# Second layer: the last query projections between sampling tiles, a narrow last tile, and last rows' maxima made inside the third layer's passes

## The chip, the cores and the metric

The kernel runs on one core of one Trainium2 chip. The core has a matmul engine (TensorE, "PE" in the profile, with its weight loads as "PEld"), a vector engine (VectorE, "DVE"), an activation engine (ScalarE, "ACT"), a general engine (GpSimd, "POOL") and a sequencer that issues DMAs (SyncE, "SP"). Each engine works through its own queue in order, and semaphores make one engine wait for another. The metric is the device time of one execution in microseconds.

## What is computed

Two images of 512 channels and 64x64 pixels go through four residual layers, each after a group normalisation `_gn`, all in fp32. The two layers that matter here, cut to their core, are

```python
# layer 1: attention to 256 sampled keys
q   = einsum('oc,bchw->bohw', w_q, x)                # projection, 512 -> 512
off = tanh(w_off2 . gelu(q[::4, ::4] * w_off1 + b_off1)) * 4
kv_feats = grid_sample_bilinear(q, grid + off)       # 16x16 samples for each of 8 heads
k, v = split(w_kv . kv_feats)
x = x + w_out . (softmax(q*scale . k) . v) + b_out
# layer 2: mixture of max pools
x = _gn(x)
s = relu(w2 . relu(w1 . mean(x) + b1) + b2)          # one number per channel
x = x_in + frac_b * maxpool(x, k_b) + frac_s * maxpool(x, k_s) + x    # k in 1,3,...,13
```

"The second layer" of the title is layer 1, "the third" is layer 2.

## The kernel before

The image is held in SBUF as X, 128 channels by 4 chunks (`KC`) by 4096 pixels; a second buffer of the same size, Y, holds what a layer makes on the way. Pixels are handled in 8 blocks (`NB`) of 512 (`TB`), that is, 8 rows of 64. [...]The two images run one after the other through all four layers, in one program. The order of the instructions on each engine is set by a scheduler that follows the order in which the Python code emits them, with priorities of its own; in places the code fixes it.

**Sampling** (`query_and_sample`, L1249). The bilinear sampling is a matmul. `query(blk)` (L1259) projects one block: for each of the 4 output chunks, 4 matmuls (`project`, the matmul is L134), then ACT evacuates the bank into Y (L1264); at the end DVE takes the absolute maximum of the block, `top` (L1267). A tile `t` is 128 pixels, two rows of the image; there are 32. For each tile:

- ACT makes |y - t| for all heads and keys (L1297), DVE turns it into the tent (L1298) and multiplies it by the tent in x, `hatx` (L1299). The result `wt` has two buffers.
- PE transposes the 4 chunks of the tile's queries (L1302) into one of four PSUM banks, ACT copies them to `q_tok` (L1305), which has two buffers as well.
- PE adds the tile to the samples in `acc`, 8 matmuls (L1308), one for each head.

An offset is at most 4 grid steps, so a tile can only touch some of the 16 rows of keys; `keys_near(t)` gives them, and L1297 to L1308 work on that slice of the keys. The first and the last tile take all 16 rows. The loop (L1287) emits the projections of block `blk + 1` ahead of the four tiles of block `blk`. After the last tile one copy takes all samples from PSUM to `feats` (L1310), from which keys and values are made (L1064, L1070).

**End of layer 1** (L1090 to L1122). The attended values of a block stand in Y. `add_output` (L1190) multiplies them by `w_out`, 4 matmuls for each output chunk (L1195), adds the result into X (L1198) and takes the statistics (L1200); L1114 aggregates a chunk's. Meanwhile the 3x3 maxima of X, the first pool of layer 2, are made into Y: `maxima_across` (L1124) makes the horizontal maxima of a block's 8 rows into `rows3` on DVE (L1132, L1134) and copies edges and the two last rows of the block before on ACT (L1131, L1133), `maxima_down` (L1138) the vertical ones on DVE (L1145, L1146, at the very end L1148). Then `pool_mixture` (L1150) turns the statistics of all channels into 7 weights per channel, a chain of small steps on PE, DVE, POOL and ACT (L1157 to L1188). The last `maxima_down`, of three chunks, is issued behind it with `issue_after`.

**Layer 2** (`pool_chunk`, L1337), once for each of the 4 chunks. 8 PSUM banks hold the chunk's image. Seven terms are added into them: term 0 is X itself, term 1 the 3x3 maxima in Y, and terms 2 to 6 are wider maxima. A term is added with 8 matmuls (L1356) by a diagonal of weights that ACT makes (L1361). A wider maximum is made from the last one by two passes of `spread_max` (L689): each is one DVE operation over the whole image (L698) and an ACT copy of its two edges (L699). The passes write in turn to the scratch image `pool_h` and to a buffer of `self.pools`, two of its own and the Y chunks that are free. Behind the last term ACT evacuates the 8 banks into X (L1398), sums squares (L1402) for the next normalisation. In the last chunk these are L1390 and L1391; there the last bank's products of terms 0 to 4 are kept back and issued during term 5, and six weight blocks of layer 3 are scaled on DVE (L978).

Of the kernel before, what the change touches and what calls it, by code (L numbers as in the profile page):

```python
# [933 lines left out]
class Net(General):  # L934
# [102 lines left out]
    def layer1(self, X, Y, d):  # L1037

        tc, nc, vec = self.tc, self.nc, self.vec
        with tc.tile_pool(name="l1", bufs=1) as sp:  # L1040
            wkv = sp.tile([P, KC, 2 * C], F32, name="wkv1")
            nc.sync.dma_start(wkv, d["w_kv1"].rearrange("(kc p) o -> p kc o", p=P))
            wq = sp.tile([P, KC, C], F32, name="wq1")
            feats = sp.tile([P, KC, NK], F32, name="feats")
            bq = sp.tile([P, KC], F32, name="bq1")
            with tc.tile_pool(name="l1a", bufs=1) as wp, \
                    tc.tile_pool(name="l1p", bufs=4, space=PSUM) as pp, \
                    tc.tile_pool(name="l1k", bufs=1, space=PSUM) as ppk:
                grid = wp.tile([P, 2, NK], F32, name="grid")
                nc.sync.dma_start(grid, d["grid"])  # L1050
                top = sp.tile([P, KC, NB], F32, name="top_q")
                self.query_and_sample(X, Y, wq, bq, grid, feats, top, wp, pp, ppk)
            self.ahead = ExitStack()
            dp = self.ahead.enter_context(tc.tile_pool(name="diags", bufs=1, side="right"))
            self.diags = cycle([dp.tile([P, P], F32, name=f"diag{i}") for i in range(2)])
            with tc.tile_pool(name="l1c", bufs=1) as late:

                keys = late.tile([P, KC, NK], F32, name="keys")
                vals = late.tile([P, 2, C], F32, name="vals")
                with tc.tile_pool(name="l1q", bufs=4, space=PSUM) as pp:  # L1060
                    for oc in range(KC):
                        ps = pp.tile([P, TB], F32, name="mm")
                        for kc in range(KC):
                            nc.tensor.matmul(ps[:, :NK], wkv[:, kc, oc * P:(oc + 1) * P],  # L1064
                                             feats[:, kc, :], start=(kc == 0), stop=(kc == KC - 1))
                        nc.scalar.mul(keys[:, oc, :], ps[:, :NK], HD ** -0.5)
                    for t in range(2):
                        ps = pp.tile([P, TB], F32, name="mm")
                        for kc in range(KC):
                            nc.tensor.matmul(ps, feats[:, kc, t * P:(t + 1) * P], wkv[:, kc, C:],  # L1070
                                             start=(kc == 0), stop=(kc == KC - 1))
                        nc.vector.tensor_copy(vals[:, t, :], ps)
                    self.product_bound(top, keys, sp, pp)
                with tc.tile_pool(name="l1b", bufs=2) as wp, \
                        tc.tile_pool(name="l1s", bufs=6, space=PSUM) as pp, \
                        tc.tile_pool(name="l1o", bufs=2, space=PSUM) as ppo:
                    st = wp.tile([P, KC, NB, 6], F32, name="gn_st1", bufs=1)
                    w1 = wp.tile([P, KC, 32], F32, name="w1", bufs=1)
                    nc.sync.dma_start(w1, d["w1"].rearrange("(kc p) e -> p kc e", p=P))
                    w2 = wp.tile([32, C], F32, name="w2", bufs=1)  # L1080
                    nc.sync.dma_start(w2, d["w2"])
                    wo = wp.tile([P, KC, C], F32, name="wo1", bufs=1)
                    nc.sync.dma_start(wo, d["w_out1"].rearrange("(kc p) o -> p kc o", p=P))
                    steps = [(blk, cc) for blk in range(NB) for cc in range(KC)]
                    part = lambda blk, cc=slice(0, KC): Y[:, cc, blk * TB:(blk + 1) * TB]
                    flat = lambda a: a.rearrange("p k o -> p (k o)")
                    probs, totals, later = {}, {}, []
                    rows3 = flat(wkv)[:, :KC * 10 * W].rearrange("p (k y x) -> p k y x", k=KC, x=W)
                    ring = cycle([a[:, n:n + TB] for a, lo, hi in (
                        (flat(wq), 0, KC), (flat(wkv), 5, 8), (flat(feats), 0, 2),  # L1090
                        (wp.tile([P, 3 * TB], F32, name="totals", bufs=1), 0, 3))
                        for n in range(lo * TB, hi * TB, TB)]).__next__
                    for i in range(len(steps) + 4 + KC):
                        if i < len(steps):
                            blk, cc = steps[i]
                            probs[i], totals[i] = self.exponentials(part(blk, cc), keys[:, cc, :],
                                                                    ring, wp, pp)
                        if 1 <= i <= len(steps):
                            blk, cc = steps[i - 1]
                            self.attended(part(blk, cc), probs.pop(i - 1),  # L1100
                                          vals[:, :, cc * P:(cc + 1) * P], ppo)
                        at = lambda n: i >= n and (i - n) % KC == KC - 1 and (i - n) // KC
                        if (blk := at(1)) is not False and blk < NB:
                            r = self.inverse_sums([totals.pop(KC * blk + n) for n in range(KC)], wp,
                                                  pp)
                        if (blk := at(2)) is not False and blk < NB:
                            self.divided(part(blk), r, pp)
                        if (blk := at(3)) is not False and blk < NB:
                            later += [(blk, oc) for oc in range(KC)]
                        if later:  # L1110
                            blk, oc = later.pop(0)
                            self.add_output(X, wo, part(blk), blk, oc, st, pp)
                            if blk == NB - 1:
                                nc.vector.bn_aggr(self.mv[:, oc, :],  # L1114
                                                  st[:, oc].rearrange("p b s -> p (b s)"))
                                self.maxima_across(X, blk, rows3, slice(oc, oc + 1))
                            elif oc == KC - 1:
                                self.maxima_across(X, blk, rows3, slice(0, KC))
                                self.maxima_down(Y, blk, rows3, slice(0, KC))
                    self.maxima_down(Y, NB - 1, rows3, slice(0, 1))  # L1120
                    with tc.issue_after(self.pool_mixture(w1, w2, wp, pp)):
                        self.maxima_down(Y, NB - 1, rows3, slice(1, KC))  # L1122

    def maxima_across(self, X, blk, h, ks):  # L1124

# [12 lines left out]
    def maxima_down(self, Y, blk, h, ks):  # L1138
# [8 lines left out]
        if blk == NB - 1:  # L1147
            nc.vector.tensor_tensor(out[:, :, W - 1], h[:, :, rows], h[:, :, rows + 1], ALU.max)  # L1148

    def pool_mixture(self, w1, w2, sp, pp):  # L1150

        nc, vec, mv = self.nc, self.vec, self.mv
# [6 lines left out]
        nc.vector.tensor_tensor(cent, mv[:, :, 0], ps[:, :KC], ALU.subtract)  # L1159
        nc.vector.tensor_tensor(var, cent, cent, ALU.mult)  # L1160
        nc.vector.tensor_tensor(var, var, mv[:, :, 1], ALU.add)
        ps = pp.tile([P, TB], F32, name="mm")
        nc.tensor.matmul(ps[:, :KC], self.grp, var, start=True, stop=True)
        nc.vector.tensor_scalar(var, ps[:, :KC], 1e-5, None, ALU.add)
# [20 lines left out]
        nc.vector.tensor_tensor(up, up, down, ALU.min)  # L1185
        nc.vector.tensor_scalar(up[:, :5], up[:, :5], 0.0, None, ALU.max)
        nc.vector.tensor_tensor(wts, up, bcast(rstd, 1, 7), ALU.mult)
        return nc.vector.scalar_tensor_tensor(c0, wts[:, 0], 1.0, rstd, ALU.add, ALU.add).ins  # L1188

    def add_output(self, X, w, att, blk, oc, st, pp):  # L1190

# [57 lines left out]
    def query_and_sample(self, X, Y, wq, bq, grid, feats, top, wp, pp, ppk):  # L1249
# [35 lines left out]
            nc.gpsimd.tensor_copy(wq[:, kc], w[:, kc])  # L1285
        in_turn(self.grid_steps(banks, bq, grid, ycoord, hatx, wp, pp), query(0))
        for blk in range(NB):  # L1287
            if blk + 1 < NB:
                in_turn(query(blk + 1))
            for t in range(blk * NT, (blk + 1) * NT):  # L1290

                near = self.keys_near(t) if 0 < t < n_t - 1 else slice(0, 16)
                some = lambda a: a.rearrange("p g (i j) -> p g i j", j=16)[:, :, :, near]
                wt = wp.tile([P, NH, NK], F32, name="wt", bufs=2)
                nw = NK // 16 * (near.stop - near.start)
# [10 lines left out]
                for g in range(NH):  # L1306
                    cc, lo = g // 2, (g % 2) * HD
                    nc.tensor.matmul(some(acc[:, :, :NK])[lo:lo + HD, cc], q[:, g * HD:(g + 1) * HD],  # L1308
                                     wt[:, g], start=(t == 0), stop=(t == n_t - 1))
        nc.vector.tensor_copy(feats, acc[:, :, :NK])  # L1310

    def keys_near(self, t):

# [23 lines left out]
    def pool_chunk(self, X, Y, cc, c0, d0, wts, sp):  # L1337
# [5 lines left out]
        if cc == 0:  # L1343
            self.scratch = sp.tile([P, N], F32, name="pool_h")
            self.pools = [sp.tile([P, N], F32, name=f"pool{i}") for i in range(2)]
        else:
            self.pools.insert(0, Y[:, cc - 1, :])
        h = image(self.scratch)
        accs, kept = self.accs, []
# [1460 lines left out]
```

## Time and profile before

| | us |
|---|---|
| median of 3 runs | 5054.05 (5054.01 to 5058.16) |
| the profiled execution's own time | 5046.35 |
| span of its trace | 5044.5 |
| PE busy | 4804.4 (95%) |
| DVE busy | 3073.6 (61%) |
| ACT busy | 1817.5 (36%) |
| POOL busy | 1848.7 (37%) |
| sampling, last block of projections begins to first key matmul, image 0 | 1183.28 to 1217.57 |
| last `w_out` matmuls begin to first pool matmul, image 0 | 1475.49 to 1509.15 |
| layer 2's matmuls L1356, image 0 | 1509.15 to 1709.4 |

The three lower rows are times from the start of the span; image 1 repeats them about 2506 us later. In a timeline a row is: start, duration, engine, line, operation, out<-in, shapes, count, and in brackets how long the engine sat idle before it and whom it waited for. An fp32 matmul of this kernel is recorded as two instructions; a transpose as one. Matmuls are pipelined, so the durations of neighbours overlap: what counts is the distance of their starts, 0.43 us for one record of 512 columns.

### The profile page before, as it was taken

How to read it: one execution, taken by the hardware profiler on the slowest of the kernel's cores; microseconds unless marked ns; L12 is line 12 of the kernel's file. 1: busy time of each engine (PE TensorE's matmuls, PEld its weight loads, DVE VectorE, ACT ScalarE, POOL GpSimd, SP SyncE). 2: the span in 40 equal slices, each digit the busy share in tenths (PEclk: the TensorE clock that was granted, in tenths of full speed). 3: DMA queues.
4: the chain of work that ended last, by engine and by line, in shares of the span. 5: the costliest groups of instructions: out<-in, count | busy, mean ns of one | idle time of the engine just before them, and what ended most of it. 6: DMA issues, size and time to landing. Idle time of an engine off the chain costs nothing. (4 is left out here: it accounts for less than half of the span.)

```text
span 5044.5 us, 48001 instructions
## 1 busy us (share of the span) xinstructions
PE 4804.4 (95%) x17027; PEld 1980.2 (39%) x17027; DVE 3073.6 (61%) x3994; ACT 1817.5 (36%) x3479; POOL 1848.7 (37%) x1218
## 2 busy tenths in 40 slices
PE   7999999999999999999999999999999999999998
PEld 3433332554334444433343333335543344444333
DVE  4267777754679533478733677777436794335776
ACT  1245655334323233322112555552443232333221
POOL 0036666501320045454500466664013201554554
PEclk9999999999999999999999999999999999999999
DMA  3035556600000000211120355565000000000111
GB/s 153 0 85 145 150 148 173 163 19 10 1 1 17 2 1 1 68 58 44 58 74 0 101 148 150 146 178 142 19 10 1 17 1 1 1 1 24 40 46 44
DMA packets 124172, 307.72 MB, mean 61 GB/s; under 512 B 20818, under 2 KB 33618, under 8 KB 122388
## 3 DMA queue, kind: packets, MB, share of 16 engines
q1 hardware_dynamic: 123924, 304.58, 20.9%
q8 instruction: 136, 2.23, 0.2%
q14 instruction: 112, 0.92, 0.1%
HBM read 256.01 MB, written 48.50 MB: 60 GB/s over the span
## 5 line engine op out<-in xcount | busy, mean ns | idle before, releaser
L134 PE MATMUL mm<-big,w 128*128 128x512 f32 x2496 | 1169.7, 611 | 30.3 <-DVE big L2404 11.8
L134 PEld LDWEIGHTS mm<-big,w 128*128 128x128 f32 x2496 | 453.3, 192 | 712.7 <-issue 550.6
L2613 POOL TENSOR_TENSOR late<-late,big 128x1024 f32<-128x1024 f32 x194 | 460.1, 2371 | 233.4 <-DVE big L2608 202.0
L2447 DVE TENSOR_TENSOR prods<-qs,big 128x1024 f32<-128x1024 f32 (+1 forms) x200 | 334.2, 1686 | 76.5 <-PE tap L2474 66.3
L1643 POOL TENSOR_TENSOR big<-big 128x512 f32<-128x512 f32 x224 | 277.7, 1272 | 219.1 <-ACT big L1634 219.1
L2608 DVE TENSOR_TENSOR big<-big,mm 128x512 f32<-128x512 f32 x388 | 254.8, 682 | 120.0 <-ACT mm L2600 117.0
L2600 ACT COPY mm<-big 128x512 f32<-128x512 f32 x432 | 248.0, 597 | 109.9 <-DMA big<-rows 62.7
L1634 ACT ACTIVATE big<-mm,ed 128x256 f32<-128x256 f32 x512 | 194.1, 490 | 233.0 <-DVE top L1630 200.3
L2518 POOL TENSOR_TENSOR late<-late 128x512 f32<-128x512 f32 x84 | 105.4, 1275 | 429.8 <-ACT late L2503 408.0
L2613 POOL TENSOR_TENSOR late<-late,tap 128x1024 f32<-128x1024 f32 x94 | 222.1, 2363 | 99.6 <-DVE tap L2608 80.6
L1446 POOL TENSOR_TENSOR wq<-prob 128x512 f32<-128x512 f32 x48 | 70.8, 1497 | 502.6 <-ACT prob L1443 502.6
L1898 PE MATMUL mm<-k,w 128*128 128x512 f32 x512 | 238.5, 610 | 12.4 <-DVE k L1891 7.4
L1630 DVE TENSOR_REDUCE top<-mm 128x1 f32<-128x512 f32 x256 | 159.0, 684 | 148.1 <-PE mm L1561 148.1
L134 PE MATMUL mm<-big,wq 128*128 128x512 f32 x512 | 232.4, 603 | 2.7 <-ACT off_t L1223 2.7
L1195 PE MATMUL mm<-big,wo 128*128 128x512 f32 x512 | 234.7, 604 | 0.0
L1608 PE MATMUL mm<-w,big 128*128 128x512 f32 x512 | 234.5, 601 | 0.0
L1356 PE MATMUL acc<-big,diag 128*128 128x512 f32 x512 | 226.8, 600 | 4.6 <-ACT diag L1361 4.6
L973 POOL TENSOR_TENSOR group_stats<-group_stats,cst 128x1 f32<-128x1 f32 (+1 forms) x20 | 12.1, 621 | 560.1 <-DVE group_stats L972 499.9
L1888 DVE RECIPROCAL psD<-psD 128x512 f32<-128x512 f32 x64 | 215.1, 3362 | 1.9
L134 PE MATMUL mm<-big,big 128*128 128x512 f32 x464 | 201.7, 594 | 0.5 <-DVE b_sr L1011 0.5
L1443 ACT ACTIVATE prob<-mm 128x512 f32<-128x512 f32 x256 | 133.0, 602 | 171.3 <-PE mm L1440 171.1
L1530 POOL TENSOR_TENSOR sq<-k 128x512 f32<-128x512 f32 x128 | 132.9, 1040 | 155.4 <-ACT k L1528 139.4
(419 smaller groups left out, 8219.4 us busy)
## 6 DMA issues: line engine op xcount, KB each, us to landing
big<-rows SPq DMA_DIRECT2D x432, 256.0 KB, 4.1
tap<-rows SPq DMA_DIRECT2D x208, 256.0 KB, 4.1
yd<-late SPq DMA_DIRECT2D x32, 512.0 KB, 3.1
lost_all<-lost SPq DMA_DIRECT2D x128, 128.0 KB, 3.1
out<-big SPq DMA_DIRECT2D x64, 256.0 KB, 2.0
big<-in_W_kv SPq DMA_DIRECT2D x8, 1024.0 KB, 10.7
rows<-late SPq DMA_DIRECT2D x64, 128.0 KB, 3.5
big<-in_x SPq DMA_DIRECT2D x32, 256.0 KB, 3.7
```

Source lines behind the costliest of these rows:

```text
L134: self.nc.tensor.matmul(ps, w[:, kc, :], X[:, kc, blk * TB:(blk + 1) * TB], start=(kc == 0), stop=(kc == KC - 1))
L1195: nc.tensor.matmul(ps, w[:, kc, oc * P:(oc + 1) * P], att[:, kc, :], start=(kc == 0), stop=(kc == KC - 1))
L1356: nc.tensor.matmul(accs[b], dg, src[:, b * TB:(b + 1) * TB], start=(j == 0), stop=(j == 6))
L1608: nc.tensor.matmul(ps, X[:, kc, lo:lo + P], wv[:, kc, :], start=(kc == 0), stop=(kc == KC - 1))
L1634: nc.scalar.activation(f[:, t, :], pS[h][i][:, t % 2, :], AF.Exp, bias=ed[:, t, 2 * cc + h:2 * cc + h + 1])
L1643: nc.gpsimd.tensor_tensor(a, a, part, ALU.add)
L1888: nc.vector.reciprocal(psD, psD)
L1898: nc.tensor.matmul(ps, self.wo[:, kc, oc * P:(oc + 1) * P], qs[:, kc, :], start=(kc == 0), stop=(kc == KC - 1))
L2447: self.nc.vector.tensor_tensor(self.pair(u, k)[:, :n].rearrange("p k (y x) -> p k y x", x=W), bcast(qs.rearrange("p (y x) -> p y x", x=W), ...
L2600: nc.scalar.copy(ps, part)
L2608: nc.vector.tensor_tensor(part.rearrange("p (y x) -> p y x", x=W), self.vx[:, y:y + self.UY // 2, dx:dx + W], ps.rearrange("p (y x) -> p y ...
L2613: nc.gpsimd.tensor_tensor(out, out, t, ALU.add)
```

## The change

In the sampling loop the projections of the last block (block 7) are no longer emitted ahead of the tiles of block 6, but one output chunk ahead of each of these four tiles. The last tile takes only its near keys, as the middle ones do. The copy from PSUM to `feats` is made in four pieces, one per chunk.

At the end of layer 1 the maxima of the last block are made for chunk 0 only, between the two parts into which `pool_mixture` is now divided; of block 6 they are made for chunks 0 and 1 only. What is missing (the last 9 rows of chunk 1, the last 17 of chunks 2 and 3) is made in layer 2 by a new function, `maxima_below`, at the start of the chunk that needs it. `issue_after` goes.

```diff
                             if blk == NB - 1:
                                 nc.vector.bn_aggr(self.mv[:, oc, :],
                                                   st[:, oc].rearrange("p b s -> p (b s)"))
-                                self.maxima_across(X, blk, rows3, slice(oc, oc + 1))
-                            elif oc == KC - 1:
+                                if oc < 2:
+                                    self.maxima_across(X, NB - 2, rows3, slice(oc, oc + 1))
+                                    self.maxima_down(Y, NB - 2, rows3, slice(oc, oc + 1))
+                            elif oc == KC - 1 and blk < NB - 2:
                                 self.maxima_across(X, blk, rows3, slice(0, KC))
                                 self.maxima_down(Y, blk, rows3, slice(0, KC))
+                    mixture = self.pool_mixture(w1, w2, wp, pp)
+                    next(mixture)
+                    self.maxima_across(X, NB - 1, rows3, slice(0, 1))
                     self.maxima_down(Y, NB - 1, rows3, slice(0, 1))
-                    with tc.issue_after(self.pool_mixture(w1, w2, wp, pp)):
-                        self.maxima_down(Y, NB - 1, rows3, slice(1, KC))
+                    next(mixture)
...
+    def maxima_below(self, x, to, h, blk):
+        nc = self.nc
+        x, to, h = (a.rearrange("p (y x) -> p y x", x=W) for a in (x, to, h))
+        y = blk * TB // W - 1
+        n = W - y
+        x, h, to = x[:, y - 1:], h[:, y - 1:], to[:, y:]
+        nc.vector.tensor_tensor(h[:, :, 1:W - 1], x[:, :, :W - 2], x[:, :, 2:], ALU.max)
+        nc.scalar.copy(h[:, :, 0:W:W - 1], x[:, :, 1:W - 1:W - 3])
+        nc.vector.tensor_tensor(h, h, x, ALU.max)
+        nc.vector.tensor_tensor(to[:, :n - 1], h[:, :n - 1], h[:, 2:], ALU.max)
+        nc.vector.tensor_tensor(to[:, :n - 1], to[:, :n - 1], h[:, 1:n], ALU.max)
+        nc.vector.tensor_tensor(to[:, n - 1], h[:, n - 1], h[:, n], ALU.max)
...
         nc.vector.tensor_tensor(var, var, mv[:, :, 1], ALU.add)
+        yield
         ps = pp.tile([P, TB], F32, name="mm")
         nc.tensor.matmul(ps[:, :KC], self.grp, var, start=True, stop=True)
...
-        return nc.vector.scalar_tensor_tensor(c0, wts[:, 0], 1.0, rstd, ALU.add, ALU.add).ins
+        nc.vector.scalar_tensor_tensor(c0, wts[:, 0], 1.0, rstd, ALU.add, ALU.add)
+        yield
...
         for blk in range(NB):
-            if blk + 1 < NB:
-                in_turn(query(blk + 1))
+            ahead = query(blk + 1) if blk + 1 < NB else iter(())
+            if blk < NB - 2:
+                in_turn(ahead)
             for t in range(blk * NT, (blk + 1) * NT):
-
-                near = self.keys_near(t) if 0 < t < n_t - 1 else slice(0, 16)
+                next(ahead, None)
+
+                near = self.keys_near(t) if t else slice(0, 16)
...
-        nc.vector.tensor_copy(feats, acc[:, :, :NK])
+            for _ in ahead:
+                pass
+        for cc in range(KC):
+            nc.vector.tensor_copy(feats[:, cc], acc[:, cc, :NK])
...
             self.pools = [sp.tile([P, N], F32, name=f"pool{i}") for i in range(2)]
         else:
+            self.maxima_below(x2, Y[:, cc, :], self.scratch, NB - 1 if cc == 1 else NB - 2)
             self.pools.insert(0, Y[:, cc - 1, :])
```

## The prediction

> **What bounds the kernel now.** First the busy shares: PE is busy 95% of the span, so time is won only where PE stands still, or where its work shrinks. Then the timeline around the two places of the change, image 0. The end of sampling, in the timeline of all engines (start, duration, engine, line, [idle before, releaser]):
>
> ```profile
> 1183.28 11.43 PE L134 MATMUL mm<-big,wq 128*128 128x512 f32 x26
> ...
> 1204.09 0.99 PE L1308 MATMUL acc<-wt,q_tok 128*64 128x112 f32 x16 [1.41 <-DVE wt L1299]
> ...
> 1207.01 2.00 ACT L1297 ACTIVATE wt<-ycoord,yneg 128x2048 f32<-128x2048 f32 x1 [0.48 <-PE acc L1308]
> ...
> 1209.04 1.23 DVE L1298 TENSOR_SCALAR wt<-wt 128x2048 f32<-128x2048 f32 x1 [1.41 <-ACT wt L1297]
> 1210.30 2.29 DVE L1299 TENSOR_TENSOR wt<-wt,hatx 128x2048 f32<-128x2048 f32 x1
> ...
> 1212.74 3.52 PE L1308 MATMUL acc<-wt,q_tok 128*64 128x256 f32 x16 [3.41 <-DVE wt L1299]
> ...
> 1216.30 1.22 DVE L1310 COPY feats<-acc 128x1024 f32<-128x1024 f32 x1 [3.70 <-PE acc L1308]
> ...
> 1217.57 7.17 PE L1064 MATMUL mm<-feats,wkv 128*128 128x256 f32 x32 [1.32 <-DVE feats L1310]
> ```
>
> PE spends its last projections in one dense block; then tiles 26 to 31 come bare, each a chain ACT tent, two DVE steps, PE. From 1197.85 to 1217.57 the windows give PE 12.19 of 19.72 us, at a granted clock of 0.74. The end of layer 1, PE alone:
>
> ```profile
> 1500.18 0.59 PE L1157 MATMUL mm<-channels_mv,cst 128*128 128x4 f32 x2 [7.26 <-DVE channels_mv L1114]
> ...
> 1509.15 15.86 PE L1356 MATMUL acc<-big,diag 128*128 128x512 f32 x32 [2.30 <-ACT diag L1361]
> 1524.84 20.97 PE L1356 MATMUL acc<-pool,diag 128*128 128x512 f32 x48
> 1547.53 7.11 PE L1356 MATMUL acc<-pool,diag 128*128 128x512 f32 x16 [1.72 <-DVE pool L698]
> 1556.35 7.11 PE L1356 MATMUL acc<-pool,diag 128*128 128x512 f32 x16 [1.72 <-DVE pool L698]
> ```
>
> PE stands 7.26 us because DVE is late with statistics: it has maxima in between (DVE timeline: L1132 2.21, L1134 2.28, L1145 2.28, L1146 2.23 us, so the second of the last block's sums, ready at 1485.8, is added at 1490.83). In layer 2 PE waits twice for a pool pass, later never. But DVE is busy 182.95 of layer 2's 200.20 us, and in chunk 1 it already waits for an edge copy that stands in ACT's queue behind the evacuations of chunk 0:
>
> ```profile
> 1566.49 4.29 DVE L698 TENSOR_TENSOR pool_h<-big 128x3968 f32<-128x3968 f32 x1 [1.49 <-ACT big L699]
> ```
>
> [...]at 1509.15 the first five weight loads are 0.86 us apart, then 0.43, which cost 2.1 us.[...]
>
> **The change, part by part**, for one image. The order of each queue is read from the built program: PE's order changes only in the sampling tail, POOL's and SP's not at all, no DMA moves; DVE and ACT change there, at the end of layer 1 and in layer 2.
>
> (a) *Sampling tail.* From 1183.28 PE has 13 projection matmuls left (0.86 each, 11.2), now with tiles 24, 25, 26 among them (4 transposes 0.45 plus 16 records 0.95 each, 4.2) and some 0.25 of waits for q_tok, which stands behind the evacuation (0.69) on ACT: the block ends at 1198.9 instead of 1194.5, three tiles further. Transposes 1.4; tile 27, whose tent is ready, runs 1200.45 to 1201.35, tile 28 to 1202.2. Then bare: tents 29 and 30 on ACT (0.94 each, two buffers, so each behind a PE tile) end 1202.35 and 1203.25; DVE, free at 1202.4 after `top`'s 2.29, makes 0.56+0.96 twice, to 1203.95 and 1205.45; PE 1204.05 and 1205.55. Tile 31 with 80 instead of 256 columns a head: tent 0.84 (from 0.94 and 1.04 at 96 and 112), starting 1205.0; DVE 0.49+0.82; PE 1207.4 to 1208.3. It had cost 2.00+1.23+2.29+3.52. A quarter of the feats copy is 0.42 (L1654, 256 columns, 421 ns), so the key matmuls start at 1208.95: 8.6 earlier. [...]0 or the 2.1 above; I take 2.1. Gain 6.5.
>
> (b) *End of layer 1.* Block 6's maxima come down from four chunks to two, block 7's to one, and stand where DVE waited. After its L1482 (1478.4) DVE has 2.6 us of maxima, then two sums and statistics (1.4 each) to 1483.9, 1.6 of maxima and a statistic, and meets the sum ready at 1485.8 in time, likewise 1489.2. The last, 1492.65, finds DVE free; 0.75+0.69+0.37 less overlap give 1494.5, and L1157 starts at 1494.6: 5.6 earlier. 0.25 more goes because L1146 and L1148 no longer stand ahead of L1159. First pool matmul: 1503.3, 5.85 earlier. The added ACT copies there are 0.25 to 0.30, next to 4 us pauses: nothing.
>
> (c) *Layer 2.* Count from its first matmul, T=0. Removed ahead of the passes: L1145, L1148, L1146 of three chunks, 3.66 us, so the first pass starts at -0.55 instead of +3.11. Added: `maxima_below`, [...]0.80+0.82+0.69+0.22+0.69=3.2 us for chunk 1 (10 rows) and 1.32+1.36+1.22+0.22+1.22=5.3 for chunks 2 and 3 (18 rows), 13.9 in all. A pass is 4.40 start to start, a term's matmuls 6.87. Chunk 0: pass 6 must wait until PE has read term 2 (22.6), +1.2; pass 10 ends 44.6, so term 6 runs 44.65 to 51.5 (before 54.1; the two stalls of 1.72 shrink to about 1.5). Chunk 1 on: queued on ACT behind eight evacuations and four squares (as the copy shown above is) there is now the edge copy of the chunk's *first* pass, and DVE's second pass waits for it: it starts 3.35 after PE has ended the chunk before (1566.49 against 1563.29, and 0.15 for the longer copy). From there to the end of pass 10 are 39.5 (chunk 2 before, less its wait), then term 6 on PE. So each chunk goes round a loop of 3.35+39.5+0.05+6.87=49.8 us, where PE alone needs 48.05: chunk 1 ends at 101.3 (before 102.2), chunk 2 at 151.1 (150.3). Chunk 3: pass 6 ends 176.35, PE waits 1.1; pass 8 ends 185.2, PE waits 2.5; term 5 and the products kept back are 26 records, 11.2, to 196.4; the six scalings L978 (2.5) now stand ahead of pass 10, which ends 196.45. The last term starts at 196.5, before at 193.2 (1702.38): 3.3 lost. The cover that would make (c) free is PE's work, and it is 1.75 too short per chunk.
>
> *Sum:* 6.5+5.85-3.3=9.05 an image, 18.1 for two. The profiled execution, 5046.35 with a span of 5044.5, would become 5028.3; the median stood 7.7 above it and is taken to move alike: 5054.05-18.1=**5036.0**.
>
> **Rivals.**
> *DVE keeps ahead in layer 2*, if edge copies get out sooner: then chunk 0 gives 2.6 more and nothing is lost, 6.5+5.85+2.6=15, twice 30: 5024. For it: DVE's 17 us of slack; against it: ACT's order.
> *The tail stays bare.* If the tiles among projections stall PE on q_tok[...], (a) gives half, 3.3: 5042. For it: 0.81 to 1.59 us pauses at tiles 26 to 30; against it: all operands of 24 to 28 are timely by (a).
> *Layer 2 eats (b) and more.* If below-steps and squares cost 3 us more by chunk 3: 2x(6.5+5.85-8.5)=7.7: 5046.
> *Slower.* The loop of (c) again, as the one bound: if the first edge copy waits for all eight squares, four more at 0.9 put 3.6 on each of three loops, and the six weight scalings of 2.5 then fall whole on the path: 3.3+10.8+2.5=16.6 against 12.35 gained, twice 4.3 lost[...]: 5063 to 5075, say 5065. It decides from 9.05 us an image, 3 us a chunk, beyond my loop. Against it: four squares stood ahead before, and stand ahead now.
> *The change doing nothing* is out: the built program has the narrow tile and the new order.
>
> **How the numbers follow.** Forecast 0.50 (own range 5030 to 5041[...]), DVE ahead 0.17, bare tail 0.14, eaten 0.13, slower 0.06. A range of 5024 to 5046 leaves about 2 in 10 outside. 0.2% is 10 us, about what a measurement of this kernel can tell from no change: faster, 5044 and less, is the first three, 0.81; same is "eaten" and a little of "slower", 0.14; slower 0.05.
>
> **What would show it.** Right: L1064 some 8 us earlier against the last projection block; L1157's wait from 7.26 to under 2; L698's second pass of chunks 1 to 3 released by ACT L699; PE waiting on L698 about 2 us at each chunk's last term, last term near 196.5 after the first matmul. Wrong: no PE wait on L698 in chunks 1 to 3 (then faster), or waits of 5 us there (then slower).

## The result and the profile after

| | before | after |
|---|---|---|
| median of 7 runs, us | 5054.05 (5050.58 to 5058.16) | 5038.71 (5037.15 to 5044.18) |
| ratio after/before, 95% interval | | 0.9969 [0.9959, 0.9978] |
| the profiled execution's own time, us | 5046.35 | 5044.18 |
| span of its trace, us | 5044.5 | 5042.3 |

The kernel became 15.3 us faster; the interval reaches from 11.1 to 20.7. The forecast was 5036.0 with 18.1 to win. But the two profiled executions differ by 2.2 us only: that of before was shorter than each of the seven runs behind its median, that of after the longest of its seven. So these two spans can't be compared; stages can. All kernels of this study have the same number of matmul records (17027), so a stage can be measured between the same records in each trace:

- A: from the record that stands 208 records ahead of the first key matmul (it belongs to a sampling tile, and starts 2.5 us before the row of 26 projections with which the prediction begins) to the first key matmul (L1064);
- B: from there, so with the key matmuls, to the first pool matmul of layer 2;
- C: from there to the first matmul of layer 2's last term;
- rest: everything else in the run but for some 50 us behind C in each image.

| us, image 0 / image 1 | A | B | C | rest |
|---|---|---|---|---|
| before | 36.83 / 36.16 | 291.57 / 291.57 | 193.24 / 193.24 | 3901.3 |
| after | 28.56 / 28.56 | 288.33 / 288.69 | 199.57 / 199.54 | 3908.4 |
| after less before | -8.27 / -7.60 | -3.24 / -2.88 | +6.33 / +6.30 | +7.1 |
| as predicted | -8.6 | -5.85 + 2.1 = -3.75 | +3.3 | 0 |

The 2.1 us that the prediction took off its gain from sampling would be paid in the key matmuls, so in B. The stages give 5.2 and 4.2 us, 9.4 in all, where the forecast said 9.05 for each image. The total came out near the forecast; the sum of its stages is half of it.

**The sampling tail.** The timeline of all engines, kernel after, image 0:

```profile
1208.42 0.88 PE L1330 MATMUL acc<-wt,q_tok 128*64 128x96 f32 x16 [0.82 <-DVE wt L1321]
...
1209.89 0.88 PE L1330 MATMUL acc<-wt,q_tok 128*64 128x96 f32 x16 [0.58 <-DVE wt L1321]
...
1211.73 0.78 PE L1330 MATMUL acc<-wt,q_tok 128*64 128x80 f32 x16 [0.97 <-DVE wt L1321]
1212.54 1.42 DVE L1335 COPY feats<-acc 128x256 f32<-128x256 f32 x4 [0.96 <-PE acc L1330]
...
1213.02 7.17 PE L1064 MATMUL mm<-feats,wkv 128*128 128x256 f32 x32 [0.52 <-DVE feats L1335]
```

The bare tiles are down to three with pauses below 1 us, the wide one (2.00 + 1.23 + 2.29 + 3.52) is gone, and the key matmuls wait 0.52 for a quarter of `feats` instead of 1.32 for all of it. They take 7.17 us, as before, 0.22 us from start to start behind the first (0.32).

**The end of layer 1.** The same view some 250 us later:

```profile
1461.50 2.94 POOL L1472 TENSOR_TENSOR wq<-prob 128x512 f32<-128x512 f32 x2 [5.70 <-ACT wkv L1137]
1461.59 1.73 DVE L1136 TENSOR_TENSOR wkv<-big 128x496 f32<-128x496 f32 x1
...
1463.41 1.57 DVE L1138 TENSOR_TENSOR wkv<-wkv,big 128x512 f32<-128x512 f32 x1
...
1466.29 0.66 DVE L1136 TENSOR_TENSOR wkv<-big 128x496 f32<-128x496 f32 x1
...
1467.66 3.36 DVE L1497 RECIPROCAL recip<-mm 128x256 f32<-128x256 f32 x2
...
1471.08 1.14 PE L1505 MATMUL mm<-recip,cst 2*128 2x512 f32 x8 [1.14 <-DVE recip L1497]
```

Block 6's horizontal maxima (L1136, L1138) stand ahead of the last reciprocals on DVE. The first pair takes 1.73 and 1.57 us, while POOL works on two inputs of its own; the second, with POOL at rest, 0.66 and 0.69. The reciprocals come late and PE stands for 1.14 us. Before, it didn't wait there, and what followed ran at full rate:

```profile
1474.42 1.14 PE L1479 MATMUL mm<-recip,cst 2*128 2x512 f32 x8
...
1475.49 17.43 PE L1195 MATMUL mm<-big,wo 128*128 128x512 f32 x40
```

What follows on PE in the kernel after, to the end of layer 2:

```profile
1472.15 19.13 PE L1215 MATMUL mm<-big,wo 128*128 128x512 f32 x40
1493.26 0.39 PE L1175 MATMUL mm<-channels_mv,cst 128*128 128x4 f32 x2 [1.98 <-DVE channels_mv L1114]
...
1501.35 16.77 PE L1382 MATMUL acc<-big,diag 128*128 128x512 f32 x32 [2.29 <-ACT diag L1387]
...
1547.16 7.10 PE L1382 MATMUL acc<-pool,diag 128*128 128x512 f32 x16 [1.58 <-DVE pool L698]
...
1597.08 7.11 PE L1382 MATMUL acc<-pool,diag 128*128 128x512 f32 x16 [1.62 <-DVE pool L698]
...
1647.02 25.13 PE L1382 MATMUL acc<-big,diag 128*128 128x512 f32 x58 [1.63 <-DVE big L698]
...
1688.14 5.22 PE L1382 MATMUL acc<-pool,diag 128*128 128x512 f32 x8 [2.43 <-DVE group_stats L972]
...
1700.92 7.03 PE L1382 MATMUL acc<-big,diag 128*128 128x512 f32 x16
```

The 7.26 us wait is down to 1.98. The last 40 `w_out` records take 19.13 us instead of 17.43: four of them run at half rate, 0.85 us from start to start instead of 0.43, behind the 1.14 us stall. Such half-rate records behind a stall are called a restart below. In layer 2 PE now waits for DVE at the last term of chunks 0, 1 and 2 (1.58, 1.62, 1.63 us), before only in chunk 0, and twice in chunk 3 (0.97 and 2.43; before once, 0.79). After the 2.43 us eight records take 5.22 us; in before, unstalled, they take 3.68. The ten passes of a chunk (L698, two for each wider maximum) are counted as pass 1 to pass 10. On DVE, in chunk 1 and at the end of chunk 3:

```profile
1557.43 4.29 DVE L698 TENSOR_TENSOR big<-pool_h 128x3968 f32<-128x3968 f32 x1 [2.79 <-ACT pool_h L699]
```

```profile
1693.06 2.46 DVE L978 TENSOR_SCALAR w<-w,group_stats 128x512 f32<-128x512 f32 x6 [0.75 <-POOL group_stats L973]
1695.45 4.28 DVE L698 TENSOR_TENSOR big<-pool_h 128x3968 f32<-128x3968 f32 x1
```

The second pass waits for ACT's edge copy, queued behind evacuations and squares (2.79 here, 0.68 in chunks 2 and 3), and the six weight scalings stand ahead of the last pass. Still, that pass ends at 1699.7 and the last term starts at 1700.92: in this profile the scalings cost nothing, since PE itself was later.

### The profile page after: what moved, and what is told of

It is laid out like the page before. It is cut to its first block, busy times and chain, and to the rows that moved or that the text cites. A ratio compares the mean times of both kernels' runs of the same rounds, so it can differ in the third digit from the quotient of the medians.

```text
span 5042.3 us, 48033 instructions
## 1 busy us (share of the span) xinstructions
PE 4811.1 (95%) x17027; PEld 1980.8 (39%) x17027; DVE 3078.9 (61%) x4020; ACT 1814.7 (36%) x3477; POOL 1858.9 (37%) x1218
## 5 line engine op out<-in xcount | busy, mean ns | idle before, releaser
L973 POOL TENSOR_TENSOR group_stats<-group_stats,cst 128x1 f32<-128x1 f32 (+1 forms) x20 | 20.2, 1027 | 564.6 <-DVE group_stats L972 508.2
```

## The experiments

| run | median, us | ratio to before [95%] | A | B | C |
|---|---|---|---|---|---|
| s_only: sampling part alone | 5035.47 | 0.9966 [0.9954, 0.9978] | 28.56 / 28.55 | 291.56 / 291.57 | 193.56 / 193.46 |
| m_only: maxima part alone | 5053.66 | 0.9995 [0.9986, 1.0003] | 36.74 / 36.46 | 287.10 / 288.22 | 199.27 / 198.17 |
| b0: after, no `maxima_below` | 5024.27 | 0.9942 [0.9929, 0.9956] | 28.55 / 28.55 | 287.00 / 288.86 | 191.87 / 191.57 |
| ds: after, squares later | 5036.63 | 0.9965 [0.9953, 0.9977] | 28.55 / 28.56 | 288.37 / 288.68 | 194.49 / 194.52 |
| w: after, maxima behind the reciprocals | 5035.39 | 0.9964 [0.9950, 0.9978] | 28.55 / 28.57 | 285.59 / 285.59 | 198.18 / 199.23 |
| dsaw: ds and w, statistics on ACT | 5027.56 | 0.9944 [0.9930, 0.9957] | 28.57 / 28.55 | 287.43 / 287.45 | 196.21 / 196.54 |
| dsawk: dsaw, kept products earlier | 5022.59 | 0.9936 [0.9922, 0.9949] | 28.55 / 28.56 | 287.42 / 285.59 | 191.96 / 191.78 |
| n_only: narrow tile alone | 5049.85 (one) | | 31.44 / 30.40 | 293.34 / 291.56 | 193.20 / 193.23 |
| i_only: projections between tiles alone | 5053.77 (one) | | 35.61 / 35.61 | 291.55 / 293.43 | 193.19 / 193.21 |
| before2: before once more | 5052.37 (one) | | 36.67 / 36.83 | 291.56 / 291.56 | 193.21 / 193.23 |

A ratio is to runs of before made along with the run, with medians from 5053.14 to 5055.69. "(one)" is a single execution, of which only the stages are used.

**The two halves.** `s_only` is before with the sampling hunks of the diff, `m_only` before with the others.

> The kernel before with the sampling part alone (last projections between the tiles, narrow last tile, feats in four pieces). Prediction on record: 6.5 us an image, 13.0 in all, 5041. Theory from the trace after: [...]8.3 and 7.6 us in the two images, 15.9 in all, 5038; block of projections to first key matmul 26.0 us in both images. Rival: the gain read from the sampling stage is partly given back behind it (the tiles moved early only shift work): under 10, over 5044.

> The kernel before with the maxima part alone (block 6 and 7 maxima of the chunks split, the rest made in layer 2). Prediction on record: (b) 5.85 less (c) 3.3, that is 2.55 us an image faster, 5049. Theory from the trace after: 3.25 won before the first pool matmul and 6.3 lost behind it, 3.1 us an image slower, 5060. Rival: the two parts help each other and the maxima part alone is neutral, 5054.

The sampling part alone gives all of A and leaves B and C as they were: 15.9 us by A over the two images (8.27 and 7.61). The maxima part alone can't be told from no change by its median; by stages it wins 4.5 and 3.4 in B and loses 6.0 and 4.9 in C, 1.6 us lost an image, half of what the theory from the trace after expected. In image 0 that is because the restart described next did not come. In image 1 the key matmuls took 8.62 us instead of 7.17, which lies in B, and C was 1.1 us shorter. C of after, m_only and w, whose layer 2 is the same code, shows why: it is 199.2 to 199.6 in the four images where half-rate records followed the 2.43 us stall, and 198.2 in the two where they didn't; there the last term waited 0.34 us for pass 10. The neutral rival was nearest, and (c) is larger than (b), which the forecast had the other way round. By medians `s_only` and the whole change can't be told apart; nothing shows that the second half helped.

`m_only` has the same 1.1 us wait at the reciprocals as the kernel after. Its PE timeline:

```profile
1475.47 1.14 PE L1500 MATMUL mm<-recip,cst 2*128 2x512 f32 x8 [1.13 <-DVE recip L1492]
1476.54 17.43 PE L1215 MATMUL mm<-big,wo 128*128 128x512 f32 x40
```

Here the 40 records run at full rate. Over after, b0, ds and m_only, two images each, the wait was followed by half-rate records in five cases and not in three, with the same code. What decides between the two was not shown. The wait was 1.12 to 1.14 us in all eight; where there was no wait (before, before2, s_only, n_only, i_only, w, dsaw and dsawk, 16 cases) all 40 records ran at full rate.

**What of the sampling part does what.** Two more runs: `near = self.keys_near(t) if t else slice(0, 16)` alone (n_only), and the generator `ahead` alone (i_only).

> The kernel before with the narrow last tile alone. By the rows of the bare last tile (2.00 + 1.23 + 2.29 + 3.52 us wide against 0.84 + 0.49 + 0.82 + 0.9 narrow) block of projections to first key matmul 28.3 instead of 34.3 us: 6.0 us an image, 5042. Rival, [...]2 us of it come back, and L1064's 32 records last 9 instead of 7.2 us.

> The kernel before with the last projections between tiles alone, last tile wide and feats in one copy. What the rows of the narrow tile (6.0) and the four pieces of feats (0.8) leave of the 8.27 us of the sampling part: 1.5 us an image, 32.8 us from block to key matmuls. Rival, on record as 'the tail stays bare': nothing, 34.3 us, since tiles 29 to 31 hang on ACT and DVE all the same.

Against A's mean of 36.6 in the four images of before, the narrow tile gives 5.2 and 6.2, the order alone 1.0. The wait ahead of the key matmuls is 0.8 shorter with the four copies, which were not run alone. With 6.2 that makes 8.0 of the 8.1 of the whole part; with 5.2 it falls short. PE's timeline of `n_only`, image 0, shows where it lost 1 us before the key matmuls and more in them:

```profile
1206.19 1.55 PE L1308 MATMUL acc<-wt,q_tok 128*64 128x96 f32 x16 [0.48 <-DVE wt L1299]
1208.42 1.55 PE L1308 MATMUL acc<-wt,q_tok 128*64 128x96 f32 x16 [0.68 <-DVE wt L1299]
1210.17 1.34 PE L1308 MATMUL acc<-wt,q_tok 128*64 128x80 f32 x16 [0.20 <-DVE wt L1299]
1212.83 8.95 PE L1064 MATMUL mm<-feats,wkv 128*128 128x256 f32 x32 [1.32 <-DVE feats L1310]
```

The tiles take 1.55 and 1.34 us instead of 0.88 and 0.78, and the key matmuls 8.95 instead of 7.17: 1.8 us more, where the prediction had charged 2.1. In image 1 of the same run the key matmuls took 7.17. In `i_only` it was image 1 that took longer (9.04). With both parts together, over the seven profiles that have them (s_only, after, b0, ds, w, dsaw, dsawk), the key matmuls took 7.17 in 11 of 14 images and 8.80 to 8.84 in the other 3.

**What layer 2 pays.** `b0` takes out the line that calls `maxima_below` for chunks 1 to 3:

```
-            self.maxima_below(x2, Y[:, cc, :], self.scratch, NB - 1 if cc == 1 else NB - 2)
```

> The kernel after without the three calls of maxima_below (it leaves out the last rows' 3x3 maxima of chunks 1 to 3). Theory that DVE's added 13.9 us are what layer 2 pays: passes keep ahead of PE, last term about 190.5 us after the first pool matmul instead of 199.6, 9 us an image, 5020.5. Rival, that the place of the edge copy in ACT's queue is what costs, not the work: only the waits change hands, last term at 196 to 197, 5032.

C falls by 7.7 and 8.0 us to 191.9 and 191.6, near the 190.5 of the first theory: the work of `maxima_below`, its DVE steps with their edge copy, is what C pays. The rival that only the copies' place matters (196 to 197) falls in this form. But how much of the 13.9 us of work shows depends on the queues, and `ds` moves nothing but those: `finish` makes the squares and statistics of a chunk within the next one.

```
+        def finish():
+            nc.scalar.mul(shift, sums[:, 0, 0:1], -1.0 / TB)
+            for b, xx in enumerate(blocks):
+                nc.scalar.activation(self.junk, xx, AF.Square, bias=shift, accum_out=sums[:, 1, b:b + 1])
...
+            if j == 2 and cc:
+                self.finish()
```

> The kernel after, with the squares of chunks 0 to 2 emitted after the next chunk's first wide maximum, so that on ACT the edge copy of the first pass stands ahead of nearly all squares, and on DVE the six scalings stand behind the last pass. Theory that ACT's order costs DVE 2.8 + 0.7 + 0.7 us an image and the scalings 2.5 more: last term at about 192 instead of 199.6 after the first pool matmul, 7 us an image, 5024.5. Rival, that DVE's work alone (49.3 us a chunk in chunks 2 and 3 against PE's 48.05) is the bound: under 2 us an image, 5035 to 5038. Third: the statistics of chunk 2 come late and stall chunk 3: slower than the kernel after.

C falls by 5.1 and 5.0 us with all of `maxima_below` in place; the waits for edge copies are gone, the scalings stand behind the last pass. It is less than the 7 of the theory. By its median, 5036.63 where 5024.5 was expected, `ds` can't be told from the kernel after. The third rival, late statistics, shows in the trace, though C did not become longer than in after. PE in chunk 3:

```profile
1672.85 0.39 PE L965 MATMUL acc<-channels_mv,cst 128*128 128x3 f32 x2 [2.17 <-DVE channels_mv L1437]
...
1686.15 0.39 PE L970 MATMUL acc<-group_stats,cst 128*128 128x3 f32 x2 [0.79 <-DVE group_stats L968]
...
1697.63 7.03 PE L1382 MATMUL acc<-big,diag 128*128 128x512 f32 x16
```

The statistics of chunk 2 are a chain of six tiny steps, spread among 4.3 us passes on DVE: it begins at 1663.86 and ends at 1681.69. Started later, its third step holds up PE by 2.17 us. The 0.79 us was there in before too.

**The reciprocals.** `w` holds the early maxima back on DVE:

```
                                 if oc < 2:
-                                    self.maxima_across(X, NB - 2, rows3, slice(oc, oc + 1))
-                                    self.maxima_down(Y, NB - 2, rows3, slice(oc, oc + 1))
+                                    with tc.issue_after(self.scaled.ins):
+                                        self.maxima_across(X, NB - 2, rows3, slice(oc, oc + 1))
+                                        self.maxima_down(Y, NB - 2, rows3, slice(oc, oc + 1))
...
-            nc.vector.tensor_tensor(att[:, cc, :], att[:, cc, :], ps, ALU.mult)
+            self.scaled = nc.vector.tensor_tensor(att[:, cc, :], att[:, cc, :], ps, ALU.mult)
```

> The kernel after, with block 6's maxima (chunks 0 and 1) held on DVE behind the last multiplication by the reciprocals. Theory that they stood ahead of the reciprocals and so cost PE 1.14 us at L1505 and, since PE had stood, up to 1.7 us of matmuls at half rate behind it: from the first key matmul to the first pool matmul 285.5 instead of 288.3 us, 2.8 us an image, 5033. Rival, that the maxima only move to where the sums of the last block wait: the wait of L1175 grows from 1.98 to 3 or more and under 1 us an image is left, 5037 to 5039.

B is 285.59 in both images, 2.74 and 3.10 less than after, and the wait of L1175 stays at 1.98. The rival falls. The median, 5035.39 where 5033 was expected, can't be told from that of after. PE's timeline of `w`, image 0:

```profile
1468.12 1.14 PE L1506 MATMUL mm<-recip,cst 2*128 2x512 f32 x8
1469.19 17.43 PE L1216 MATMUL mm<-big,wo 128*128 128x512 f32 x40
1488.60 0.38 PE L1176 MATMUL mm<-channels_mv,cst 128*128 128x4 f32 x2 [1.98 <-DVE channels_mv L1114]
```

The pair of maxima that had taken 1.73 and 1.57 us now takes 1.25 and 1.28 us for two operations each. In the kernel after, the same operation took 1.73 us beside POOL's and 0.66 without. `w` takes the maxima away from the reciprocals and from POOL's operations at once, so what each of the two costs PE is not separated.

**Both, and the statistics.** In `dsaw`, which has both edits, ACT makes the statistics of chunks 0 to 2 except for one sum on DVE:

```
-            nc.vector.tensor_reduce(total, sums, AX.X, ALU.add)
-            nc.vector.tensor_scalar(total, total, 1.0 / N, None, ALU.mult)
...
+            nc.vector.tensor_reduce(total[:, :2], sums, AX.X, ALU.add)
+            nc.scalar.mul(mv, total[:, :2], 1.0 / N)
+            nc.scalar.activation(total[:, 2:], mv[:, 0:1], AF.Square, bias=shift)
+            nc.scalar.activation(mv[:, 1:2], total[:, 2:], AF.Identity, scale=-1.0, bias=mv[:, 1:2])
```

The group statistics in chunk 3 (L966 to L968) are made on ACT in the same way.

> Run ds (squares behind the next chunk's first edge copies) with the same hold as in run w, and with the small statistics of chunks 0 to 2 made on ACT but for one sum each, so that they no longer stand one pass apart on DVE. Theory: ds left PE waiting 2.2 and 0.8 us for statistics in chunk 3 while pass 10 was ready 2.9 us before the last term; without that the last term comes at about 191.6 us after the first pool matmul (ds 194.5, after 199.6), and with 2.8 us from the hold 9.6 us an image against the kernel after, 5019.5. Rival, that DVE's passes slip again behind the added ACT work, or layer 3 gives it back at its first weights: as ds and w add up, 6.7 us an image, 5025.

Its time is nearer to the rival's, and what was expected of C did not come. B is 287.4 in spite of the hold because the key matmuls took 8.82 and 8.84 us in the two images instead of 7.17. The waits at the statistics are gone, yet C is 196.2, worse than in `ds`. PE's timeline of `dsaw` in chunk 3:

```profile
1679.87 6.23 PE L1390 MATMUL acc<-pool,diag 128*128 128x512 f32 x10 [2.46 <-DVE pool L698]
...
1692.80 7.03 PE L1390 MATMUL acc<-big,diag 128*128 128x512 f32 x16
```

PE, no longer late, stood 2.46 us for pass 8 instead, and its records after that were at half rate (10 in 6.23; in dsawk 10 in 4.45). Behind pass 8 there are 26 records before the last term, so the last term came 4.3 us after pass 10. The stall hadn't been removed, only moved to where in both images a restart followed; behind the 2.17 us of `ds` none did. `dsawk` fills that gap with matmuls that were ready, and takes the second statistics matmul one term earlier:

```
-                while kept and j == 5 and b == 3:
+                while kept and (j, b) in ((4, 6), (5, 3)):
...
-            if len(kept) in (3, 5):
+            if len(kept) in (3, 4):
```

and the weight scalings are held behind the last pass with `issue_after`.

> Run dsaw, with four of the last bank's kept products issued already in term 4, the second statistics matmul one term earlier, and the six weight scalings held behind the last pass. Theory: in dsaw the last term came 4.3 us after pass 10, because PE stood 2.5 us for pass 8 and then had 26 records to do before it; with the kept products in that gap, 18 records stay behind pass 8 and the last term starts with the end of pass 10, at about 192 instead of 196.2 us after the first pool matmul: 4 us an image, 5019. Rival, that the bank kept for statistics comes free too late (its reader on DVE stands behind pass 7) and PE waits there instead: under 1.5 us an image, 5025 or more.

PE in chunk 3 of `dsawk`:

```profile
1671.06 8.85 PE L1390 MATMUL acc<-big,diag 128*128 128x512 f32 x20 [0.18 <-DVE big L698]
1679.75 4.45 PE L1390 MATMUL acc<-pool,diag 128*128 128x512 f32 x10
...
1688.67 7.11 PE L1390 MATMUL acc<-big,diag 128*128 128x512 f32 x16 [0.17 <-DVE big L698]
```

C is 191.96 and 191.78 against the 192 expected, and the same as in `b0`, where the work is left out; the rival, at most 1.5 us won, falls. Whether C would be shorter still without the work and with this order was not run. By the ratio the kernel is 32 us faster than before (26 to 39 by the interval), and its interval lies clear of that of the change. Its median, 5022.59, is the lowest of the study, though its interval meets that of `dsaw`. It is 3.6 us above the expected 5019. In its profile image 0 lost 1.6 us in the key matmuls (8.80 instead of 7.17) and 3.0 us at the start of layer 3 (49.87 instead of 46.90 from the last term to a fixed record), where eight records took 5.66 us instead of 3.60; image 1 lost neither.

**Before once more.**

> The kernel before once more, for a second profile. If the stages decide, the times of the stages in question agree with the first profile within 0.3 us (34.3 us from the last block of projections to the key matmuls, 291.6 from there to the first pool matmul, 193.2 to the last term), while its own time lies nearer to the medians, 5051 to 5058, because of stages that the change does not touch. Rival, that the gain seen in medians beyond the stages comes from the changed stages after all: then they differ here.

B and C agree within 0.03 us. A, expected within 0.3, differs by 0.16 and 0.67, and the rest of the run took 3905.4 instead of 3901.3 us. The first theory stands in the main: of the 6.0 us between the two executions, 0.5 lie in A, 1.5 at the start of layer 3 behind C, and 4.1 in the rest.

## Why the prediction was right or wrong

The total was right: 15.3 us measured, 18.1 predicted, and 5038.71 lies inside both ranges. That is in good part luck: the stages named in the prediction give 9.4 us, half of the forecast, and the median fell by 6 us more for a reason that no trace shows. Of the steps, one was better than its price and two were worse:

*(a) Sampling: gain 8.3 and 7.6, predicted 6.5.* The working up to "8.6 earlier" held: the built order, the bare tiles and the quarter copy are in the trace as priced. The term that was mis-sized is the charge at the key matmuls, "0 or the 2.1 above; I take 2.1", an estimate from the half-rate records at the start of layer 2. It exists (1.8 us in one image of n_only), but with both parts it came in 3 images of 14, so its expected size was about 0.4. A wide last tile did not rule it out: i_only has the wide tile and took 9.04 us in one image of two, m_only has it in the old order and took 8.62 in image 1. Whether both parts together show it less often than n_only and i_only can't be said from so few images.

*(b) End of layer 1: gain 3.2 and 2.9, predicted 5.85.* The failed step is that block 6's maxima "stand where DVE waited". Their horizontal half stood ahead of the reciprocals, an instruction that the working didn't look at; its first pair took 1.73 and 1.57 us beside POOL, where the second took 0.66 and 0.69. That cost PE 1.14 us and, in five cases of eight, a restart of 1.7. With them moved behind, run w has 291.57 - 285.59 = 5.98: the rest of the step's arithmetic, and its prediction of the wait (under 2; 1.98), was right.

*(c) Layer 2: loss 6.3, predicted 3.3.* The mechanism was as described: the five operations of `maxima_below` took 0.80, 0.82, 0.69, 0.22 and 0.68 us in chunk 1 and 1.32, 1.36, 1.22, 0.22 and 1.22 in chunks 2 and 3, within 0.01 of the author's estimate; the second passes were released by ACT L699, PE waited at the last term of chunks 0 to 2, and the chunks followed each other at 49.9 us (predicted 49.8). Two terms were too small. Chunk 0 ended at 52.75, predicted 51.5: its first 32 records took 16.6 instead of 15.7 us, and pass 6 waited 2.34 for PE, predicted 1.2. Chunk 3 took 199.57 - 152.6 = 47.0, predicted 45.4: the stall of 2.43, foreseen as 2.5, was followed by half-rate records, 5.22 - 3.68 = 1.5. In both the charge left out is half-rate matmuls, which the prediction had put in at the key matmuls instead. The scalings ahead of pass 10 were foreseen, and only where no restart came (C of 198.2) was that pass the last to be ready.

*The rivals.* By stages "Layer 2 eats (b) and more" is what happened: it put (b) and (c) together at 2.65 us lost an image, and 3.1 and 3.4 were lost in the two images (3.2 and 2.9 gained, 6.3 paid). Its 5046 is too slow by what (a) gave beyond its price, 1.4 us an image, and by the medians' surplus. "DVE keeps ahead" needed the edge copies sooner, and in ds, where they come sooner and the scalings later, C is 5 us an image shorter. "The tail stays bare" comes near for the order alone (1.0 us), not for the whole part. The slower loop, with all eight squares ahead, did not come; four stood there, as argued.

*What stays open.* The stages give 9.4 us and the medians 15.3, with 11.1 as the interval's lower end. The rest of the run differs between profiles of kernels that are the same there, from 3901 to 3910 us, which is larger than the 6 us in question, but nothing here shows whether the medians' surplus is chance or has a cause in the other layers. It is not put down to the change's parts.

## What to carry to other kernels

When work is moved to where an engine idles, list what stands right behind it in that queue, whoever is waiting for that, and what runs beside it: here two DVE operations took 1.73 and 1.57 us beside a two-input POOL operation, 0.66 and 0.69 without. A removed stall can move to the next late operand: in chunk 3 it went from the statistics to a pass before ready matmuls filled it, and only then was C as short as without the added work. And a stall of 1 to 2.5 us of PE should be priced with the chance of a half-rate restart: 1.4 to 3.0 us more where one came, here in five of eight cases behind 1.1 us and in four of six behind 2.43.

## What the runs showed of the hardware

- Half-rate matmuls came after stalls as short as 1.13 us, in five of eight cases with the same code, and not in the other three; after 2.43 us, in four of six. The restarts seen cost 1.4 to 3.0 us; at 1.7, four records of 512 columns ran at 0.85 instead of 0.43 us. Such steps also separate executions in stages that no change touches: from layer 2's last term to a fixed record of layer 3, before took 46.83 us and before2 48.35 in image 0.
- Two-input DVE operations of 496 and 512 columns took 1.73 and 1.57 us beside a two-input POOL operation, 0.66 and 0.69 without.
- POOL's L973, 3 columns, took 4.89 us in after, where DVE ran a 4.29 us pass beside it, and 0.85 in before, where DVE waited for it.
